# Layer 2 of a four-layer graph kernel: rel times (x Wvᵀ), with transposes by VectorE and DMA

## The chip, the cores and the metric

The kernel runs on one core of a Trainium2 chip. The metric is the device time in microseconds (us); each quoted time of the kernel is the median of several runs. All data and all matrix products are fp32.

## The reference, cut to what matters

There are 128 graphs of 128 nodes with 512 features. Four layers follow one another, each closed by a layer norm. The change is in layer 2, and it also touches how layer 3 moves its attention matrix.

```python
# layer 0: x = layernorm(x + norm_adj (x W0) + bias)
# layer 1: W1 = W2 = adj, so its term is constant over a row of x; the layer norm
# takes it out, and all that is left is a factor on the variance (the 1 + EPS of step vaw)
# layer 2
q = x @ Wq.T;  k = x @ Wk.T;  v = x @ Wv.T
rel = adj.T[None] * (q @ k.transpose(0, 2, 1))
rel = rel / norm(rel, axis=2, keepdims=True)
x = layernorm(x + rel @ v)
# layer 3
h = x @ W;  s1 = h @ a[:512];  s2 = h @ a[512:]
e = leaky_relu(s1[:, :, None] + s2[:, None, :], 0.2) * adj
att = softmax(e, axis=2)
x = layernorm(x + elu(att @ h + beta * h))
```

## The kernel before, in words

The 128 graphs go through in 32 groups of four (`GB = 4`). A group's `x` is one tile of 128 partitions (nodes) by 4 graphs by 512 features and stays in SBUF from its load to its store.

**The big products.** Each layer has products of a group's 512 rows with a 512x512 weight: `w` (layer 0), `z` (layer 2, x times gq = Wq^T Wk, giving the left factor of rel), `v` (layer 2, with Wv^T) and `k` (layer 3). Class `Product` (the matmul is line 525) does each in seven half-size products of 2x2 blocks instead of eight. They are numbered 1, 2, 5, 7, 6, 3, 4 in order of execution, need sums of blocks of the left operand (tile `S`, four sums) and of the weight (made once), and are combined afterwards by adds: `d` steps on VectorE (line 417), `t` and `c` copies out of PSUM on ScalarE (line 414), `u` steps on GpSimd (line 420). One product is 28 matmuls of 256 columns; in fp32 each shows as two records, so 56 passes.

**The left operands.** The product contracts over features, so x must stand with features on the partitions. Class `Left` gets that free of charge: `y` is x^T nadj^T, `u` is x^T rel^T and `v` (of steps `h`) is x^T att^T, each in 16 matmuls of 128 columns (line 581; 32 passes), with x as the stationary operand. Class `Squares` gives x^T itself for `z`: VectorE transposes 32x32 blocks (`xt`, line 480), then `xd` issues 16 DMAs of 64 KB that put the blocks in place (line 491). The sums of `y` and `x` are made by GpSimd (`sy`, `sx`), those of `u` and `v` by VectorE straight from PSUM (`su`, `sh`).

**Layer 2 before.** `r` makes rel from z and x^T (line 669, 16 matmuls); `rm` multiplies by adj^T; `sq` and `rp` give the row norms; `rs` scales rel by them on ScalarE; `rt` transposes rel on TensorE through PSUM (line 699) and `crt` copies it out; `u` is x^T rel^T; then the product `v` with Wv^T is added onto x.

**Layer 3 before.** `sc` makes the scores s1 and s2 on VectorE; `pe` spreads s2 over the partitions by four TensorE transposes (line 725); `pl`, `ej`, `ei`, `ex`, `rd`, `so` make the softmax; `at` transposes it on TensorE (line 764); `cat` (on VectorE) copies it out and adds beta times the identity; `h` and product `k` follow, and the elu steps `ee`, `em`, `ea`.

**The order.** It is written out as three strings: `HEAD` for the first groups, `TURN` repeated once for each group, and `TAIL` for the last. `5.w1` is step `w1` of group 5, counted from a base that grows by one at each turn. Each engine, and SyncE's DMA queue (SP) with them, executes its own share of the list strictly in that order; a step that waits holds all later ones of its engine. TensorE's order in a turn of before is `z w rt r pe u v at y h k`, for groups one to four apart. PSUM gives six rotating banks to these products; in SBUF the transposed left operands (tag `aT`) rotate over three buffers.

Of the kernel before, what the change touches and what calls it, by code (L numbers as in the profile page):

```python
# [48 lines left out]
FIRST = 5  # L50
LAST = -4
# [4 lines left out]
0.dw7 0.bi00 0.w3 0.tw 0.bi11 1.ld 0.w4 0.bi01 0.uw10 0.dw3 s.g0 0.uw01 0.dw4 0.uw11 0.stw0  # L56
0.stw1 s.g1 s.cg0 0.stw2 0.stw3 s.s30 0.vaw s.q00 0.pow s.g2 s.cg1 s.q01 0.nbw s.q02 0.apw0
s.q03 0.apw1 2.ld 3.ld 0.xt0 4.ld 0.apw2 s.q10 s.g3 0.apw3 0.xt1 s.cg2 0.xt2 0.xt3 s.q11 0.xd
s.q12 1.y10 s.cg3 s.q13 1.y00 1.cy10 s.sg0 1.y11 1.cy00 s.sg2 s.sg1 1.y01 1.cy11 s.sg3 1.w1
1.cy01 s.bi 1.sy0 1.w2 s.s32 1.dw1 1.sy1 1.w5 1.dw2 1.sy2 s.s31 1.w7 1.dw5 1.sy3 1.w6 s.s33  # L60
1.dw7 1.bi10 1.w3 1.tw 0.sx0 0.sx1 1.w4 1.dw3 0.sx2 0.z1 1.dw4 1.bi00 0.z2 0.cz1 0.sx3 1.bi11
0.z5 0.dz2 1.bi01 0.z7 0.cz5 1.uw10 0.z6 1.uw01 0.dz7 1.uw11 1.stw0 0.z3 0.tz 1.stw1 0.uz11
1.stw2 0.z4 1.stw3 0.dz3 2.y10 1.vaw 0.dz4 1.pow 2.y00 2.cy10 2.bi10 1.nbw 2.y11 2.cy00 1.apw0
2.y01 2.sy1 1.apw1 1.xt0 0.r0 1.apw2 1.xt1 2.bi00 0.r1 1.apw3 1.xt2 0.r2 2.bi11 2.cy01 1.xt3
2.cy11 0.r3 2.bi01 2.w1 1.xd 0.rm 2.sy0 0.sq0 0.sq1 2.w2 2.dw1 0.sq2 2.sy2 0.sq3 0.rp 2.w5 2.dw2
2.sy3 0.rs0 0.rs1 2.w7 2.dw5 0.rs2 0.rs3 2.w6 2.dw7 2.w3 2.tw 2.uw01 2.w4 2.uw10 2.dw3 2.stw0
2.uw11 0.rt 2.dw4 1.z1 0.crt 2.stw1 1.sx0 2.stw2 1.z2 1.cz1 1.sx1 2.stw3 2.vaw 1.sx2 1.z5 1.dz2
2.pow 1.z7 1.cz5 1.sx3 2.nbw 2.apw0 2.apw1 2.xt0 1.z6 1.dz7 2.apw2 2.xt1 2.apw3 1.z3 2.xt2 1.tz
2.xt3 1.uz11 2.xd 1.z4 1.dz3 0.u10 1.dz4 0.u00 0.cu10 0.u11 0.cu00 0.su1 0.u01 0.cu11 0.su0 1.r0
0.cu01 0.su2 1.r1 0.su3 1.r2 1.r3 s.t0 1.rm s.t1 s.ct0 s.t2 s.ct1 s.t3 s.ct2 s.wa s.ct3 1.sq0  # L70
s.sv0 1.sq1 0.v1 s.sv2 1.sq2 1.sq3 s.sv1 1.rp s.sv3 0.v2 0.dv1 2.sx0 1.rs0 1.rs1 1.rs2 0.v5
0.dv2 1.rs3 2.sx1 2.sx2 0.v7 0.dv5 2.sx3 0.v6 0.dv7 0.v3 0.tv 0.uv01 0.v4 0.uv10 0.dv3 0.stv0
0.uv11 1.rt 0.dv4 1.crt 0.stv1 1.u10 0.stv2 1.u00 1.cu10 0.stv3 1.u11 1.cu00 0.vav 1.su1 0.pov
1.u01 1.cu11 1.su0 2.z1 1.cu01 0.nbv 1.su2 0.apv0 1.su3 0.apv1 2.z2 0.sc00 2.cz1 0.sc01 0.apv2
2.z5 0.sc10 0.apv3 0.sc11 2.z7 0.sc20 2.cz5 0.sc21 0.sc30 2.z6 2.dz7 0.sc31 2.z3 2.tz 2.dz2
2.uz11 2.z4 2.dz3 0.pe 2.dz4 2.r0 0.pl0 0.pl1 2.r1 0.pl2 0.pl3 2.r2 0.ej 0.ei 2.r3 0.ex0 1.v1
2.rm 0.ex1 2.sq0 2.sq1 1.v2 1.dv1 2.sq2 2.sq3 0.ex2 2.rp 1.v5 0.ex3 1.dv2 2.rs0 0.rd 0.so 2.rs1
2.rs2 1.v7 1.dv5 2.rs3 1.v6 1.dv7 1.v3 1.tv 1.uv01 1.v4 1.uv10 1.dv3 1.stv0 1.uv11 0.at 1.dv4
2.rt 3.y10 0.cat 2.crt 1.stv1 3.y00 3.cy10 3.bi10 1.stv2 3.y11 3.cy00 3.bi00 1.stv3 3.y01 3.cy11
1.vav 3.sy0 0.h10 3.cy01 0.h00 0.ch10 3.sy1 0.h11 0.ch00 3.sy2 0.sh1 0.h01 0.ch11 0.sh0 2.u10  # L80
0.ch01 3.bi11 0.sh2 2.u00 2.cu10 0.sh3 3.sy3 2.u11 2.cu00 2.su1 2.u01 3.bi01 2.cu11 2.su0 3.w1
2.cu01 1.pov 2.su2 2.su3 3.w2 3.dw1 1.nbv 1.apv0 3.w5 3.dw2 1.apv1 1.sc00 1.apv2 1.sc01 3.w7
1.apv3 3.dw5 1.sc10 3.w6 3.dw7 1.sc11 3.w3 1.sc20 3.tw 3.uw01 1.sc21 1.sc30 3.w4 3.uw10 3.dw3
1.sc31 3.uw11 4.y10 3.dw4 4.y00 4.cy10 3.stw0 4.bi10 4.y11 3.stw1 4.cy00 4.bi00 4.y01 3.stw2
4.cy11 0.k1 3.stw3 4.sy0 4.cy01 3.vaw 3.pow 0.k2 0.ck1 4.sy1 3.nbw 3.apw0 0.k5 3.apw1 0.dk2
4.sy2 3.xt0 3.apw2 0.em00 3.apw3 0.k7 3.xt1 4.sy3 0.ck5 3.xt2 0.ee00 4.bi11 3.xt3 0.k6 0.dk7
4.bi01 0.k3 0.tk 0.ea00 0.uk11 0.k4 0.dk3 0.ee01 0.em01 0.ee11 0.em11 1.pe 3.xd 4.w1 1.pl0 0.dk4
1.pl1 0.ea01 1.pl2 1.pl3 0.ea11 4.w2 0.ee10 4.dw1 1.ej 4.w5 0.em10 1.ei 0.ea10 1.ex0 4.w7 1.ex1
4.dw5 1.ex2 0.stk0 1.ex3 4.w6 4.dw7 1.rd 0.stk1 4.w3 4.tw 1.so 0.stk2 4.uw01 4.w4 0.stk3 4.uw10
4.dw2 0.vak 3.z1 3.sx0 4.dw3 4.dw4 3.sx1 4.stw0 3.z2 3.cz1 4.stw1 3.sx2 3.z5 3.dz2 0.pok 3.sx3  # L90
0.nbk 3.z7 3.cz5 0.apk0 4.uw11 0.apk1 0.fin0 3.z6 3.dz7 0.apk2 0.fin1 4.stw2 0.apk3 0.fin2
4.stw3 3.z3 3.tz 0.fin3 4.vaw 3.uz11 3.z4 3.dz3 4.pow 4.nbw 2.v1 5.ld 3.dz4 4.apw0 4.apw1 4.xt0
2.v2 4.apw2 2.dv1 4.xt1 4.apw3 4.xt2 2.v5 4.xt3 2.dv2 2.v7 2.dv5 2.v6 2.dv7 2.v3 2.tv 2.uv01
2.v4 2.uv10 2.dv3 2.stv0 2.uv11 3.r0 4.xd 2.dv4 3.r1 2.stv1 3.r2 2.stv2 3.r3 2.stv3 1.at 2.vav
3.rm 2.pov 5.y10 1.cat 3.sq0 5.y00 5.bi10 5.cy10 2.nbv 3.sq1 5.y11 5.cy00 5.bi00 5.y01 3.sq2
5.cy11 5.sy1 1.h10 5.cy01 3.sq3 1.h00 5.sy0 1.ch10 1.h11 1.ch00 3.rp 2.apv0 1.sh1 1.h01 1.ch11
2.sc00 5.sy2 1.k1 1.ch01 1.sh0 3.rs0 5.bi11 1.sh2 3.rs1 3.rs2 1.k2 2.sc01 1.ck1 4.sx0 3.rs3
1.sh3 2.apv1 1.k5 1.dk2 4.sx1 2.apv2 2.sc10 2.apv3 2.sc11 4.sx2 1.k7 1.ck5 2.sc20 1.ee00 5.sy3
2.sc21 1.k6 1.dk7 4.sx3 2.sc30 1.k3 1.tk 2.sc31 5.bi01 1.em00 1.k4 1.dk3 1.uk11 1.ee01 1.ea00
4.z1 1.dk4 1.ee11 1.em01 4.z2 4.cz1 1.em11 1.ea01 1.em10 4.z5 1.ee10 4.dz2 1.ea11 4.z7 4.cz5  # L100
1.ea10 1.stk0 4.z6 4.dz7 1.stk1 1.stk2 4.z3 4.tz 4.uz11 1.stk3 1.vak 4.z4 4.dz3 1.pok 1.nbk
1.apk0 5.w1 4.dz4 1.apk1 1.fin0 1.apk2 1.fin1 5.w2 5.dw1 1.apk3 1.fin2 1.fin3 5.w5 5.dw2 5.w7
5.dw5 6.ld 5.w6 5.dw7 5.w3 5.tw 5.uw01 5.w4 5.uw10 5.dw3 5.stw0 5.uw11 3.rt 5.dw4 4.r0 3.crt
5.stw1 4.r1 5.stw2 4.r2 5.stw3 4.r3 5.vaw 5.pow 2.pe 4.rm 3.u10 2.pl0 5.nbw 4.sq0 3.u00 3.cu10
2.pl1 3.u11 3.cu00 2.pl2 3.u01 3.su1 3.cu11 3.v1 2.pl3 3.su0 3.cu01 3.su2 5.apw0 2.ej 3.v2
5.apw1 3.dv1 5.apw2 3.su3 5.apw3 3.v5 2.ei 4.sq1 5.xt0 2.ex0 3.dv2 3.v7 2.ex1 3.dv5 2.ex2 5.xt1
2.ex3 3.v6 5.xt2 4.sq2 4.sq3 3.dv7 4.rp 2.rd 5.xt3 3.v3 3.tv 2.so 5.xd 4.rs0 4.rs1 3.uv01 4.rs2
3.v4 4.rs3 3.uv10 3.dv3 3.stv0 2.at 3.uv11 6.y10 2.cat 6.y00 3.dv4 6.cy10 6.bi10 3.stv1 6.y11
6.cy00 6.bi00 3.stv2 6.y01 6.cy11 3.stv3 2.h10 6.cy01 6.sy0 3.vav 2.h00 2.ch10 6.sy1 2.h11
2.ch00 2.sh1 6.sy2 2.h01 2.ch11 2.sh0 2.k1 2.ch01 3.pov 2.sh2 2.sh3 6.sy3 2.k2 2.ck1 3.nbv  # L110
3.apv0 5.sx0 3.apv1 3.sc00 2.k5 5.sx1 3.apv2 3.sc01 3.apv3 3.sc10 5.sx2 2.k7 2.ck5 3.sc11 3.sc20
6.bi11 2.k6 2.dk7 5.sx3 3.sc21 3.sc30 2.k3 2.tk 6.bi01 3.sc31 2.dk2 2.uk11 2.k4 2.dk3 2.ee00
2.em00 2.ee11
"""
TURN = """
4.z1 1.dk4 1.em11 1.em01 4.z2 4.cz1 1.ea00 1.ea11 1.ee01 4.z5 4.dz2 1.ee10 1.em10 1.ea01 4.z7
4.cz5 1.ea10 1.stk0 4.z6 4.dz7 1.stk1 4.z3 1.stk2 4.tz 4.uz11 1.stk3 4.z4 4.dz3 1.vak 1.pok 5.w1
4.dz4 1.nbk 1.apk0 5.w2 5.dw1 1.apk1 1.fin0 1.apk2 1.fin1 1.apk3 5.w5 1.fin2 5.dw2 1.fin3 5.w7
5.dw5 5.w6 5.dw7 6.ld 5.w3 5.tw 5.uw01 5.w4 5.uw10 5.dw3 5.stw0 5.uw11 3.rt 5.dw4 4.r0 3.crt
5.stw1 4.r1 5.stw2 4.r2 5.stw3 4.r3 5.vaw 5.pow 2.pe 4.rm 3.u10 2.pl0 5.nbw 4.sq0 3.u00 3.cu10  # L120
2.pl1 3.u11 3.cu00 2.pl2 3.u01 3.su1 3.cu11 3.v1 2.pl3 3.su0 3.cu01 3.su2 5.apw0 2.ej 3.v2
5.apw1 3.dv1 5.apw2 3.su3 5.apw3 3.v5 2.ei 4.sq1 5.xt0 2.ex0 3.dv2 3.v7 2.ex1 3.dv5 2.ex2 5.xt1
2.ex3 3.v6 5.xt2 4.sq2 4.sq3 3.dv7 4.rp 2.rd 5.xt3 3.v3 3.tv 2.so 5.xd 4.rs0 4.rs1 3.uv01 4.rs2
3.v4 4.rs3 3.uv10 3.dv3 3.stv0 2.at 3.uv11 6.y10 2.cat 6.y00 3.dv4 6.cy10 6.bi10 3.stv1 6.y11
6.cy00 6.bi00 3.stv2 6.y01 6.cy11 3.stv3 2.h10 6.cy01 6.sy0 3.vav 2.h00 2.ch10 6.sy1 2.h11
2.ch00 2.sh1 6.sy2 2.h01 2.ch11 2.sh0 2.k1 2.ch01 3.pov 2.sh2 2.sh3 6.sy3 2.k2 2.ck1 3.nbv
3.apv0 5.sx0 3.apv1 3.sc00 2.k5 5.sx1 3.apv2 3.sc01 3.apv3 3.sc10 5.sx2 2.k7 2.ck5 3.sc11 3.sc20
6.bi11 2.k6 2.dk7 5.sx3 3.sc21 3.sc30 2.k3 2.tk 6.bi01 3.sc31 2.dk2 2.uk11 2.k4 2.dk3 2.ee00
2.em00 2.ee11
"""  # L130
TAIL = """
# [59 lines left out]
6.stk3 7.uk11 7.dk2 7.k4 6.vak 7.ee00 7.dk3 6.pok 7.ee11 7.em11 6.nbk 7.dk4 6.apk0 7.em00 6.apk1  # L191
6.fin0 7.em01 6.apk2 6.fin1 7.ea00 6.apk3 6.fin2 7.ea11 7.ee01 6.fin3 7.em10 7.ee10 7.ea01
7.ea10 7.stk0 7.stk1 7.stk2 7.stk3 7.vak 7.pok 7.nbk 7.apk0 7.apk1 7.fin0 7.apk2 7.fin1 7.apk3
7.fin2 7.fin3
"""


@with_exitstack
def kernel(
# [213 lines left out]
    def copy(o, i):  # L413
        nc.scalar.copy(o, i)  # L414
# [465 lines left out]
```

## Time and profile before

| What | us |
|---|---|
| median of 3 runs (2092.33 to 2092.88) | 2092.64 |
| the profiled execution | 2092.67 |
| its span, first to last instruction | 2090.8 |
| TensorE busy | 2067.4 |
| VectorE busy | 1474.3 |
| GpSimd busy | 928.3 |
| ScalarE busy | 917.9 |
| DMA queue of SP, share of 16 engines | 17.9% |
| mean granted TensorE clock | 0.997 |

1.87 us of the profiled execution lie outside the span. The profile page has the busy time of each engine, the chain of work that ended last (followed back from the last instruction; each step is either what released the next or the instruction before it on its engine), groups of equal instructions with their busy and idle time, and DMA issues with the time from issue to landing. The timeline lists runs of equal instructions in order. A group's "mean ns of one" is the latency of one instruction; where instructions overlap, as matmuls do, the time that one adds is the length of a run divided by its count.

### The profile page before, as it was taken

The page shows a single profiled execution, that of the slowest core. Times are in us where ns is not written, and L with a number is a line of the kernel's source. Part 1 is how long each engine was busy: PE and PEld are TensorE (multiplying, and loading weights), DVE is VectorE, ACT ScalarE, POOL GpSimd, SP SyncE. Part 2 cuts the span into 40 slices and gives each one's busy share as a digit, 9 for nine tenths or more (in the row PEclk, how much of TensorE's full clock was granted, in tenths as well). Part 3 has the DMA queues.
Part 4 walks back from the last instruction along what each step waited for, and adds up shares of the span by engine and source line. Part 5 has one row for each costly group of instructions (what it writes and reads, how often), then busy time and mean ns, then how long its engine had stood idle before and what let it go on. Part 6 is the DMA issues. An engine that isn't in the chain of part 4 may idle for free.

```text
span 2090.8 us, 32011 instructions
## 1 busy us (share of the span) xinstructions
PE 2067.4 (99%) x11706; PEld 1871.8 (90%) x11706; DVE 1474.3 (71%) x2984; ACT 917.9 (44%) x1961; POOL 928.3 (44%) x776
## 2 busy tenths in 40 slices
PE   9999999999999999999999999999999999999996
PEld 6989999999998989999999989899999999899886
DVE  5568766777766677666777666776767766678777
ACT  2344444435444444444354444444443444444455
POOL 5636553354543445533545434455335454346311
PEclk9999999999999999999999999999999999999998
DMA  7101221121121111211212212112112122121102
GB/s 238 35 7 21 61 61 57 45 62 28 54 61 46 56 42 41 61 55 47 62 24 58 61 45 57 42 40 61 54 48 61 21 61 61 44 59 21 26 16 81
DMA packets 112445, 108.85 MB, mean 52 GB/s; under 512 B 11040, under 2 KB 76704, under 8 KB 112288
## 3 DMA queue, kind: packets, MB, share of 16 engines
q1 hardware_dynamic: 112288, 106.80, 17.9%
q8 instruction: 93, 1.52, 0.3%
q14 instruction: 64, 0.52, 0.1%
HBM read 39.65 MB, written 33.55 MB: 35 GB/s over the span
## 4 chain that ended last, share of the span: by engine, by line
PE 98%; DVE 1%; issue 0%; ACT 0%; POOL 0%; DMA 0%; POOLq 0%; ACTq 0%; DVEq 0%
PE p_v L525 19%; PE p_z L525 19%; PE p_w L525 18%; PE p_k L525 18%; PE pu L581 6%; PE pr L669 5%; PE py L581 5%; PE pv L581 5%; PE pg L355 1%; PE prt L699 1%; PE pe L725 1%; PE pat L764 1%; ACT x L629 0%; DVE st_v L607 0%; DMA adj_sb<-in_adj_dram 0%
## 5 line engine op out<-in xcount | busy, mean ns | idle before, releaser
L417 DVE TENSOR_TENSOR x<-p_w,x 128x512 f32<-128x512 f32 x192 | 132.0, 688 | 204.7 <-PE p_w L525 124.0
L420 POOL TENSOR_TENSOR x<-x,t_w 128x512 f32<-128x512 f32 x96 | 119.3, 1270 | 257.7 <-ACT t_w L414 256.9
L417 DVE TENSOR_TENSOR x<-p_v,x 128x512 f32<-128x512 f32 x192 | 130.1, 678 | 84.5 <-POOL x L420 59.6
L710 DVE SCALAR_TENSOR_TENSOR prod<-x,wa_bc 128x512 f32<-128x512 f32 x256 | 161.0, 681 | 21.5 <-ACT x L629 21.5
L420 POOL TENSOR_TENSOR zT<-zT,t_z 128x512 f32<-128x512 f32 x32 | 40.6, 1268 | 293.8 <-ACT t_z L414 288.3
L525 PE MATMUL p_w<-w_t,S_y 128*128 128x256 f32 x768 | 171.0, 379 | 0.0
L525 PE MATMUL p_v<-wvT_t,S_u 128*128 128x256 f32 x768 | 171.0, 379 | 0.0
L525 PE MATMUL p_k<-w_t,S_v 128*128 128x256 f32 x768 | 171.0, 379 | 0.0
L525 PE MATMUL p_z<-S_x,gq_t 128*128 128x256 f32 x768 | 171.0, 379 | 0.0
L420 POOL TENSOR_TENSOR x<-x,t_v 128x512 f32<-128x512 f32 x96 | 119.2, 1269 | 112.4 <-ACT t_v L414 112.4
L420 POOL TENSOR_TENSOR x<-x,bias_bc 128x512 f32<-128x512 f32 x128 | 162.5, 1281 | 13.2 <-PE py L581 12.3
L525 PEld LDWEIGHTS p_v<-wvT_t,S_u 128*128 128x128 f32 x768 | 146.2, 190 | 19.6
L525 PEld LDWEIGHTS p_w<-w_t,S_y 128*128 128x128 f32 x768 | 146.2, 190 | 19.6
L525 PEld LDWEIGHTS p_k<-w_t,S_v 128*128 128x128 f32 x768 | 146.2, 190 | 19.6
L525 PEld LDWEIGHTS p_z<-S_x,gq_t 128*128 128x128 f32 x768 | 146.2, 190 | 19.6
L424 POOL TENSOR_TENSOR r_n<-n,minus_half 128x4 f32<-128x4 f32 x32 | 32.3, 1009 | 281.7 <-ACT sq L685 281.7
L629 ACT ACTIVATE x<-x,nb,r_k 128x512 f32<-128x512 f32 x128 | 94.4, 803 | 101.8 <-DVE nb L623 101.8
L581 PE MATMUL py<-nadjT,x 128*128 128x128 f32 x1024 | 121.9, 279 | 0.4 <-DVE nadjT L348 0.4
L581 PE MATMUL pu<-relT,x 128*128 128x128 f32 x1024 | 119.9, 276 | 2.4 <-ACT relT L414 2.4
L581 PEld LDWEIGHTS py<-nadjT,x 128*128 128x128 f32 x1024 | 119.3, 195 | 1.4 <-DVE nadjT L348 0.8
L581 PE MATMUL pv<-attT,x 128*128 128x128 f32 x1024 | 119.6, 275 | 0.4 <-DVE attT L417 0.4
L581 PEld LDWEIGHTS pu<-relT,x 128*128 128x128 f32 x1024 | 116.9, 192 | 3.2 <-ACT relT L414 3.1
(1028 smaller groups left out, 4729.0 us busy)
## 6 DMA issues: line engine op xcount, KB each, us to landing
out_dram<-x SPq DMA_DIRECT2D x128, 256.0 KB, 2.1
x<-in_x_dram SPq DMA_DIRECT2D x31, 1024.0 KB, 5.2
x<-in_x_dram SPq DMA_DIRECT2D x2, 512.0 KB, 4.6
w<-in_L_gnn_weight_dram SPq DMA_DIRECT2D x1, 1024.0 KB, 7.1
wq_sb<-in_L_gnn_Wq_dram SPq DMA_DIRECT2D x1, 1024.0 KB, 10.4
wk_sb<-in_L_gnn_Wk_dram SPq DMA_DIRECT2D x1, 1024.0 KB, 12.4
wv_sb<-in_L_gnn_Wv_dram SPq DMA_DIRECT2D x1, 1024.0 KB, 15.4
w<-in_L_gnn_W_dram SPq DMA_DIRECT2D x1, 1024.0 KB, 16.9
```

The lines of the kernel that those rows point to most:

```text
L355: nc.tensor.matmul(wide(pg), lhsT=wq_sb[:, ec, bass.ts(gc, P)], rhs=wk_sb[:, ec, :], start=(ec == 0), stop=(ec == KC - 1),)
L417: nc.vector.tensor_tensor(o, a, b, f)
L420: nc.gpsimd.tensor_tensor(o, a, b, f)
L424: nc.gpsimd.tensor_tensor(r, v, minus_half, ALU.pow)
L525: nc.tensor.matmul(ps[:, j, :], lhsT=lhsT, rhs=rhs, start=(i not in ONTO and j == 0 and kc == 0), stop=(j == 1 and kc == 1), skip_group_ch ...
L581: nc.tensor.matmul(o, lhsT=self.x_chunk(b, kc), rhs=rhs, start=True, stop=True)
L629: nc.scalar.activation(xt, xt, AF.Identity, bias=self.nb[k][:, b : b + 1], scale=self.rstd[k][:, b : b + 1],)
L669: nc.tensor.matmul(self.pr[:, b, :], lhsT=self.zT[:, fc, b, :], rhs=self.xT.chunk(b, fc), start=(fc == 0), stop=(fc == KC - 1),)
L699: nc.tensor.transpose(self.prt[:, b, :], self.rel[:, b, :], ident)
L710: nc.vector.scalar_tensor_tensor(prod, self.x[:, b, :], 1.0, wide(wa_bc[k]), ALU.mult, ALU.mult, accum_out=self.s[:, k, b : b + 1],)
L725: nc.tensor.transpose(self.pse[:, b, :], s2, ident)
L764: nc.tensor.transpose(self.pat[:, b, :], self.e[:, b, :], ident)
```

## The change

Layer 2 is computed as rel (x Wv^T) in place of (rel x) Wv^T. The product `v` now takes x^T as its left operand, the same tile and the same four sums `S` as `z`, and its result goes to a tile of its own (`whole["v"]`, tag `vC`). Then four matmuls `f`, one per graph, with rel^T as stationary operand and 512 columns of that tile moving, give the layer's output, and `fa` on VectorE scales it by the row norm and adds it onto x in one instruction. Steps `u`, `cu`, `su`, `rs`, `uv10` and `uv01` are gone.

rel and att are transposed without TensorE: VectorE transposes 32x32 blocks (`rt`, `at`), one DMA writes the result to DRAM (`wr`, `aw`), and four DMAs of 32 partitions read it back in place (`cr`, `cat`). s2 is written to DRAM (`pw`) and read back spread over all partitions (`pe`). beta times the identity is now added in `so`, four instructions. x^T is laid out so that two feature chunks alternate element by element: the sums read contiguous blocks, and a matmul that takes one chunk reads every second element. The DMAs of `xd` move runs of 64 elements where they moved runs of 128. Tiles of pool `mid` have one buffer where they had two. The three order strings are new; 21 turns lie between a head of four groups and a tail of seven, where 23 lay between five and four.

```diff
 TURN = """
+4.z1 5.cy01 2.em01 2.em10 4.z2 4.cz1 3.pe 2.ea11 5.sy0 2.ee01 4.z5 4.dz2 5.sy1 4.z7 4.cz5 2.ea01
+3.pl0 5.sy2 2.stk0 2.ee10 2.stk1 4.z6 3.pl1 5.bi10 3.pl2 4.dz7 3.pl3 3.ej 4.z3 4.tz 2.ea10 3.ei
+4.uz11 4.z4 4.dz3 3.ex0 5.sy3 3.ex1 2.stk2 3.ex2 4.r0 2.stk3 3.ex3 5.bi00 4.dz4 4.r1 3.rd 5.bi11
+2.vak 4.r2 4.r3 3.so0 2.pok 3.so1 5.w1 3.so2 3.so3 4.rm 5.bi01 3.at 4.sq0 5.w2 4.sq1 5.dw1 3.aw
+4.sq2 2.nbk 4.sq3 2.apk0 5.w5 4.rp 5.dw2 2.apk1 2.fin0 2.apk2 2.fin1 4.rt 5.w7 2.apk3 3.cat
+5.dw5 5.w6 5.dw7 4.wr 5.w3 5.tw 2.fin2 5.uw01 2.fin3 5.w4 5.uw10 5.dw3 4.cr 5.stw0 5.uw11 3.h10
+5.dw4 3.h00 5.stw1 3.ch10 3.h11 5.stw2 3.ch00 7.ld 3.h01 5.stw3 3.ch11 3.sh0 4.v1 3.ch01 5.vaw
+3.sh1 5.pow 3.sh2 4.v2 4.cv1 5.nbw 3.sh3 5.apw0 5.apw1 5.xt0 4.v5 4.dv2 5.apw2 5.xt1 5.apw3 4.v7
+5.xt2 4.cv5 5.xt3 4.v6 4.dv7 4.v3 4.tv 4.uv11 4.v4 4.dv3 4.f0 5.xd 4.dv4 4.f1 4.fa0 4.stv0 4.f2
+4.fa1 4.f3 4.fa2 3.k1 4.fa3 4.stv1 3.k2 3.ck1 4.stv2 4.stv3 3.k5 3.dk2 4.vav 3.ee00 3.em00 4.pov
+3.k7 3.ck5 3.ea00 4.nbv 4.apv0 3.k6 3.dk7 4.apv1 4.sc00 4.apv2 4.sc01 3.k3 4.apv3 4.sc10 5.sx0
+3.tk 4.sc11 3.k4 5.sx1 4.sc20 4.sc21 5.sx2 6.y10 4.sc30 6.y00 6.cy10 4.sc31 3.uk11 3.dk3 6.y11
+4.pw 6.cy00 5.sx3 3.dk4 3.ee11 6.y01 6.cy11 3.em11
 """
...
-    mid = ctx.enter_context(tc.tile_pool(name="mid", bufs=2))
+    mid = ctx.enter_context(tc.tile_pool(name="mid", bufs=1))
+    dram = ctx.enter_context(tc.tile_pool(name="dram", bufs=2, space=bass.MemoryType.DRAM))
...
         def square(self, b, x):
             nc.vector.transpose(
-                self.u[:, b].rearrange("p q k r -> p k q r"),
-                x.rearrange("p (k q a) -> p k q a", k=KC, q=4),
+                self.u[:, :, b].rearrange("p h t r e -> p h e t r"),
+                x.rearrange("p (h e t a) -> p h e t a", h=2, e=2, t=4),
             )
         def move(self):
-            self.aT = big.tile([P, GB, 4, KC, 32], F32, tag="aT", name=f"{self.name}T")
+            self.aT = big.tile([P, 2, GB, P, 2], F32, tag="aT", name=f"{self.name}T")
             for q in range(4):
                 for to in range(4):
-                    nc.sync.dma_start(out=self.aT[rows(to), :, q], in_=self.u[rows(q), :, to])
+                    nc.sync.dma_start(
+                        out=self.aT[rows(to), :, :, rows(q), :], in_=self.u[rows(q), :, :, to]
+                    )
...
+    def across(o, u, name):
+        d = dram.tile([P, 4, P], F32, tag="sq", name=f"d_{name}")
+        nc.sync.dma_start(out=d, in_=u)
+        yield
+        by_t = d.rearrange("(q i) t x -> t i q x", q=4)
+        for t in range(4):
+            nc.sync.dma_start(out=o[rows(t)], in_=by_t[t])
+        yield
...
-                "v": Product(f"v_{g}", self.u, "v"),
+                "v": Product(f"v_{g}", self.xT, "v"),
...
-        def rs(self, b):
-            r = self.rel[:, b, :]
-            nc.scalar.activation(r, r, AF.Copy, scale=self.rnorm[:, b : b + 1])
-
         def rt(self):
-            self.prt = bank(f"prt_{self.g}")
-            for b in range(GB):
-                nc.tensor.transpose(self.prt[:, b, :], self.rel[:, b, :], ident)
-
-        def crt(self):
-            self.relT = mid.tile([P, GB, P], F32, tag="relT", name=f"relT_{self.g}", bufs=1)
-            copy(self.relT, self.prt)
+            self.ru = mid.tile([P, 4, 32, GB], F32, tag="ru", name=f"ru_{self.g}")
+            nc.vector.transpose(
+                self.ru.rearrange("p t r b -> p b t r"),
+                self.rel.rearrange("p b (t a) -> p b t a", t=4),
+            )
+        def wr(self):
+            self.relT = mid.tile([P, 4, 32, GB], F32, tag="relT", name=f"relT_{self.g}")
+            flat = lambda t: t.rearrange("p t r b -> p t (r b)")
+            self.way = across(flat(self.relT), flat(self.ru), f"r_{self.g}")
+            next(self.way)
+        def cr(self):
+            next(self.way)
+        def f(self, b):
+            nc.tensor.matmul(
+                self.pf[b],
+                lhsT=self.relT.rearrange("p q r b -> p b (q r)")[:, b],
+                rhs=self.whole["v"][:, b, :],
+                start=True,
+                stop=True,
+            )
+        def fa(self, b):
+            xt = self.x[:, b, :]
+            nc.vector.scalar_tensor_tensor(
+                xt, self.pf[b], self.rnorm[:, b : b + 1], xt, ALU.mult, ALU.add
+            )
...
+        def pw(self):
+            self.d = dram.tile([P, GB], F32, tag="s2", name=f"d_s_{self.g}")
+            nc.sync.dma_start(out=self.d, in_=self.s[:, 1, :])
         def pe(self):
-            self.pse = bank(f"pe_{self.g}")
-            for b in range(GB):
-                s2 = self.s[:, 1, b : b + 1].to_broadcast([P, P])
-                nc.tensor.transpose(self.pse[:, b, :], s2, ident)
+            self.s2 = mid.tile([P, P, GB], F32, tag="ru", name=f"s2_{self.g}")
+            flat = self.d.rearrange("j b -> (j b)").partition_broadcast(P)
+            nc.sync.dma_start(out=self.s2.rearrange("p j b -> p (j b)"), in_=flat)
...
-        def so(self):
-            tt(self.e, self.e, self.rden.unsqueeze(2).to_broadcast([P, GB, P]), ALU.mult)
+        def so(self, b):
+            nc.vector.scalar_tensor_tensor(
+                self.e[:, b, :], self.e[:, b, :], self.rden[:, b : b + 1], beta_i, ALU.mult, ALU.add
+            )
         def at(self):
-            self.pat = bank(f"pat_{self.g}")
-            for b in range(GB):
-                nc.tensor.transpose(self.pat[:, b, :], self.e[:, b, :], ident)
+            self.au = mid.tile([P, 4, GB, 32], F32, tag="ru", name=f"au_{self.g}")
+            nc.vector.transpose(
+                self.au.rearrange("p t b r -> p b t r"),
+                self.e.rearrange("p b (t a) -> p b t a", t=4),
+            )
         def cat(self):
-            self.attT = mid.tile([P, GB, P], F32, tag="attT", name=f"attT_{self.g}", bufs=1)
-            tt(self.attT, self.pat, beta_i.unsqueeze(1).to_broadcast([P, GB, P]))
+            next(self.way)
```

## The prediction

> **What bounds the kernel now.** I read the page's busy times first, then the chain of work that ended last, then the stages of one turn.
>
> ```profile
> PE 2067.4 (99%) x11706; PEld 1871.8 (90%) x11706; DVE 1474.3 (71%) x2984; ACT 917.9 (44%) x1961; POOL 928.3 (44%) x776
> ...
> PE 98%; DVE 1%; issue 0%; ACT 0%; POOL 0%; DMA 0%; POOLq 0%; ACTq 0%; DVEq 0%
> ```
>
> TensorE is in the chain for 98% of the span, and no other engine comes near it. A busy TensorE alone proves little, as matmuls are pipelined; so I look for gaps. All waits of TensorE's matmuls that the list of waits shows come to under 9 us, most of it before the first product. Then I take the pieces of the chain in order of time, one turn:
>
> ```profile
> 1043.33 3.57 PE pr L669 x32
> ...
> 1050.91 12.09 PE p_v L525 x56
> 1063.44 3.57 PE py L581 x32
> 1067.01 3.57 PE pv L581 x32
> 1070.58 12.09 PE p_k L525 x56
> 1082.67 12.09 PE p_z L525 x56
> 1094.76 12.09 PE p_w L525 x56
> ```
>
> The p_v of the next turn starts at 1114.87, so a turn lasts 63.96 us. It is full: four products of 12.09 are 48.36, four stages of 3.57 (r, u, y, h) are 14.28, three sets of transposes at 0.434 are 1.30: 63.94. So a microsecond less of TensorE work is a microsecond less of time, as long as nothing else becomes late. The price of a pass is the run divided by its count: 12.09/56 = 216 ns at 256 columns, 3.57/32 = 112 ns at 128. At 512 columns the setup's product gives it:
>
> ```profile
> 23.68 13.73 PE pg L355 x32
> ```
>
> 13.73/32 = 429 ns.
>
> [...] 2.0 to 2.1 us from issue to landing for the stores of 256 KB and the moves of 64 KB. [...] loads of 190 ns lie inside passes that follow each other at 216 ns.
>
> **The change part by part, for one group.** TensorE, on the path:
>
> - removed: u, 32 passes, 3.57 us; the transposes rt, pe and at, 3 x 0.434 = 1.30 us. Sum 4.87.
> - added: f, four matmuls of 512 columns, 8 passes x 0.429 = 3.43 us. The same columns stream as in u; what is saved there is the fixed part of 24 passes, 0.14 us.
> - kept: w, z, v, k, y, h, r at their lengths. z and r now read x^T at every second element, and v loads its weights so. Unknown cost; from below nothing, since the same number of columns streams. From above, half rate: 12.09 + 3.57 = 15.7 us. I take zero [...]. The weight loads for v could last 216 ns before they show, and f's, at every fourth element, 429 ns.
>
> Net -1.44 us, so a turn of 62.5. For 32 groups: 32 x 1.44 = 46.1 us.
>
> VectorE, beside TensorE: removed are four sums su (0.61 us each as one follows another, from the timeline), two of six adds dv, so and cat: 8 x 0.61 = 4.9. Added are four fa and two transposes at 0.61 (3.7) and four so of 128 columns. No such row exists: at least 0.15 us each, as for the smallest operations, at most the 0.61 of four times the size; 0.6 to 2.4, I take 1.1. Net -0.1: it stays near 45 us of a turn of 62.5, against 45.16 of 63.95. The transposes write with gaps of 8 or 16 bytes; at double time they add 6 x 0.61 = 3.7 us, still below 50. ScalarE loses four cu and crt (0.49 each) and four rs (0.32), gains two cv: -2.8. GpSimd loses two uv: -2.5. Neither bounds anything, so these are worth nothing.
>
> SP's queue gains 12 DMAs a group (wr, aw, pw, pe one each, cr and cat four each) beside the 16 of xd, four stores and one load:
>
> ```profile
> 995.80 11.06 SPq L491 DMA_DIRECT2D x_16T<-sq_x  x16
> ...
> 1032.47 2.45 SPq L638 DMA_DIRECT2D out_dram<-x  x4
> ```
>
> An issue takes about 0.7 us, so 33 take 23 us of 62.5. What matters is when they land. I set t = 0 at z1 of a turn; TensorE then runs z to 12.1, r to 15.7, w to 27.8, h to 31.3, v to 43.4, f to 46.9, k to 59.0, y to 62.5.
>
> - rel: r ends at 15.7, rm and rt by about 20.5 (rt waits for the DMA aw to let go of tag ru), wr lands at 23, cr, behind two stores, by 26 to 28. f starts at 43.4: 15 us to spare. f0 also needs dv3 and f2 dv4; each has one product step (1.73) or two f (1.7) of cover.
> - att: f ends at 46.9, so fa, the statistics, apv and sc on VectorE end at about 59.5 (dk7 waits until k7 at 53.8). pw and pe, one issue and 2.0 us each, land at about 64.5, which is 2.0 of the next turn. pl stands behind cz5 (5.3) on ScalarE anyway, so this round trip is hidden with 3 us. ej, ei, ex, rd, so end at 14.6; at waits behind rm (r ends at 15.7) and ends at 17.0; aw lands at 19.1; cat issues behind stores fin0 and fin1, held by apk0 and apk1, and lands at 24.4. h starts at 27.8: 3.4 us to spare. This is the tightest chain. A late cat delays h and everything behind it on TensorE.
> - x^T: xd now waits for v4, because x^T of the group before is in use until then (three buffers aT, three tiles in a turn). So 43.5 to 54.5 for 16 issues, landed at 56.5; sx at 1.25 us each. z1 starts at 62.5: 6 us to spare, and z5 needs the first sum only at 66.
>
> The single buffers of pool mid cost nothing as I see it: t is used once a product, 12 us apart; prod and sq by one engine in order; only ex makes each ee wait for the ea before it, 0.6 us on ScalarE, which is more than half idle. Of the new waits, rt behind aw holds VectorE's dw5, dw7 and dw3; xd behind v4 holds only pw on SP, which is not ready before 59.5.
>
> Head and tail do the same steps in other orders. Before, TensorE starts at 5.57, and after its last product 20.8 us of elu, norm and stores follow; both stay. In the tail the last group has, between f and h, 47.0 us of TensorE steps (h and k of three groups) as cover, where a turn has 43.4, but 43 us of VectorE steps where a turn has 30. I allow 1.5 us for gaps, with 0 and 10 as ends.
>
> **Sum.** 2092.67 (profiled execution; 2090.8 span and 1.87 around it; the median, 2092.64, is the same) - 46.1 + 1.5 = **2048 us**.
>
> **The rivals.**
>
> *The DMA round trip through DRAM is late.* If att lands d us after 27.8, or the last groups wait, TensorE stands still by d each turn. For: 3.4 us is little, and the write and the reads are new forms; reads of 512-byte runs could take longer than 2.0. Against: xd moves runs of 512 bytes with 2.0 us. With each of aw and cat at 4.5 us, 0.9 of aw's delay is hidden behind fin1, and cat lands at 24.4 + 1.6 + 2.5 = 28.5: 0.7 late, 31 x 0.7 = 22 us, 2070. It decides from 3.4 us on.
>
> *x^T arrives late; this one ends slower.* Runs of 64 elements double the pieces of each xd DMA. If its issues double too, to a period of 1.4 us, 15 x 1.4 + 2.5 = 23.5 us after 43.4 is 66.9, and z1 is 4.4 us late in each turn: 31 x 4.4 = 136, 2184 us. It costs nothing up to a period of (19.0 - 2.5)/15 = 1.1 us and eats the whole gain from (20.4 - 2.5)/15 = 1.2. Against: the number of pieces does not set the issue time here; a store of 128 pieces takes 0.33 us, a load of 512 pieces 0.39, an xd of 128 pieces 0.6. DMA engines are busy 43% in that stretch, so twice the packets would just fit.
>
> *The strided reads cost.* z and r at half rate: 32 x 15.7 = 502 us, about 2550. The gain is gone at 1.44/15.7, a 9% slowdown. [...]
>
> *The work was not on the path.* If TensorE's passes waited for weight loads, fewer of them would not help: 2092. Against: the turn adds up from passes to 0.02 us.
>
> **How the numbers follow.** Forecast 0.72, with its own range 2043 (1.5 us of allowance and some of the old gaps gone, 0.14 us more from f) to 2060; late round trip 0.15 (2060 to 2085); x^T late 0.06; strided reads 0.05; not on the path 0.02. About 0.2%, 4 us, is what a measurement tells from no change. Faster: 0.72 + 0.15 = 0.87, less 0.01 for a round trip worse than 2088, 0.86; same 0.02 + 0.01 = 0.03; slower 0.06 + 0.05 = 0.11. For 8 in 10 the range takes in the forecast and the better half of the late round trip: 2043 to 2073.
>
> **What would show it.** Right: a turn of 62.5 us, z and r at 216 and 112 ns a pass, runs of f at 3.43, no transposes of rel, e and s on TensorE, VectorE at 45 us a turn. Wrong: TensorE waiting on attT before h (round trip), on x^T or S_x before z (xd's issue above 1.1 us), longer passes in p_z and pr alone (strides), or gaps in the tail above 10 us.

## The result and the profile after

| What | before | after |
|---|---|---|
| median, us | 2092.64 | 2068.68 (2068.12 to 2069.11) |
| ratio to before, 95% interval | | 0.9885 (0.9868 to 0.9903) |
| profiled execution, us | 2092.67 | 2068.12 |
| its span, us | 2090.8 | 2066.2 |
| one turn, us | 63.96 | 63.18 |

The change gains 24 us. The forecast was 2048 with a range of 2043 to 2073, a gain of 44.6. So the sign and the range held, and close to half of the gain is missing. The first two lines to read on the page after are again the busy times and the shares of the chain of work that ended last.

```profile
PE 2041.6 (99%) x10554; PEld 1800.8 (87%) x10554; DVE 1610.6 (78%) x3048; ACT 844.1 (41%) x1737; POOL 915.1 (44%) x712
...
PE 95%; DVE 2%; issue 1%; ACT 1%; DMA 0%; SPq 0%; POOL 0%; POOLq 0%; ACTq 0%; DVEq 0%
```

TensorE is still busy for 99% of the span, with a tenth fewer instructions; VectorE rose by 136 us. The missing gain is therefore not idle time of TensorE. The list of waits confirms it: TensorE's matmuls wait 7.7 us in all, none of it for attT or relT. So the time must lie in the length of TensorE's pieces. The chain of the kernel after, in order of time, has for one turn (start, length, engine, what it writes, line, count of passes):

```profile
1004.17 3.57 PE pv L617 x32
1007.74 12.10 PE p_v L564 x56
1023.28 12.09 PE p_k L564 x56
1035.37 3.57 PE py L617 x32
1038.94 12.69 PE p_z L564 x56
1051.63 3.63 PE pr L703 x32
1055.26 12.09 PE p_w L564 x56
1067.35 3.57 PE pv L617 x32
```

The stretch without a line, 1019.84 to 1023.28, is f with 3.44 us. Two pieces are longer than before: p_z has 12.69 instead of 12.09 us, and pr has 3.63 instead of 3.57. These are the two that now read x^T at every second element. The product p_v, which takes every second element as weights, kept its length within 0.01 us. The groups of equal instructions say the same of single instructions (busy us, then the mean ns of one):

```profile
L564 PE MATMUL p_z<-S_x,gq_t 128*128 128x256 f32 x768 | 179.2, 387 | 0.0
...
L564 PE MATMUL p_v<-wvT_t,S_x 128*128 128x256 f32 x768 | 171.0, 379 | 0.0
```

Both are 768 matmul records of 256 columns with the same S_x; only the role of S_x differs. As the moving operand it costs 179.2 us, as weights 171.0, which is also what p_z cost before.

The account closes: 12.69 - 12.09 = 0.60 and 3.63 - 3.57 = 0.06 make 0.66 us a turn, and 32 x 0.66 = 21.1 us. The profiled execution of before less the 46.1 us of the forecast plus these 21.1 is 2092.67 - 46.1 + 21.1 = 2067.7; measured is 2068.12.

### The profile page after: what moved, and what is told of

Same layout as the page of the kernel before. It is cut to its first block, busy times and chain, and to the rows that moved or that the text cites. A ratio compares the mean times of both kernels' runs of the same rounds, so it can differ in the third digit from the quotient of the medians.

```text
span 2066.2 us, 29797 instructions
## 1 busy us (share of the span) xinstructions
PE 2041.6 (99%) x10554; PEld 1800.8 (87%) x10554; DVE 1610.6 (78%) x3048; ACT 844.1 (41%) x1737; POOL 915.1 (44%) x712
## 4 chain that ended last, share of the span: by engine, by line
PE 95%; DVE 2%; issue 1%; ACT 1%; DMA 0%; SPq 0%; POOL 0%; POOLq 0%; ACTq 0%; DVEq 0%
PE p_z L564 19%; PE p_v L564 19%; PE p_w L564 18%; PE p_k L564 17%; PE pr L703 6%; PE py L617 5%; PE pv L617 5%; PE pf L746 5%; PE pg L379 1%; DVE x L852 0%; DMA x<-in_x_dram 0%; SPq L518 0%; ACT x L665 0%; DVE prod L765 0%; DVE st_k L643 0%
## 5 line engine op out<-in xcount | busy, mean ns | idle before, releaser
L564 PE MATMUL p_z<-S_x,gq_t 128*128 128x256 f32 x768 | 179.2, 387 | 0.0
L564 PE MATMUL p_w<-w_t,S_y 128*128 128x256 f32 x768 | 171.0, 379 | 0.0
L564 PE MATMUL p_v<-wvT_t,S_x 128*128 128x256 f32 x768 | 171.0, 379 | 0.0
L448 POOL TENSOR_TENSOR r_v<-v,minus_half 128x4 f32<-128x4 f32 x32 | 43.7, 1366 | 287.0 <-DVE v L652 286.8
L564 PEld LDWEIGHTS p_z<-S_x,gq_t 128*128 128x128 f32 x768 | 144.1, 188 | 29.9
L564 PEld LDWEIGHTS p_v<-wvT_t,S_x 128*128 128x128 f32 x768 | 150.8, 196 | 14.9
L844 ACT ACTIVATE ex<-C_k 128x512 f32<-128x512 f32 x128 | 80.8, 631 | 146.3 <-DVE x L852 85.1
L848 DVE SCALAR_TENSOR_TENSOR x<-C_k,x 128x512 f32<-128x512 f32 x128 | 136.0, 1096 | 0.0
L441 DVE TENSOR_TENSOR C_v<-p_v,t_v 128x512 f32<-128x512 f32 x64 | 44.3, 692 | 113.9 <-PE p_v L564 113.9
L852 DVE SCALAR_TENSOR_TENSOR x<-ex,x 128x512 f32<-128x512 f32 x128 | 124.9, 976 | 10.2 <-ACT ex L844 5.2
L444 POOL TENSOR_TENSOR C_v<-C_v,t_v 128x512 f32<-128x512 f32 x32 | 40.5, 1266 | 201.1 <-ACT t_v L438 196.1
L665 ACT ACTIVATE x<-x,nb,r_v 128x512 f32<-128x512 f32 x128 | 94.4, 804 | 69.2 <-DVE nb L659 69.2
L617 PEld LDWEIGHTS pv<-attT,x 128*128 128x128 f32 x1024 | 119.4, 192 | 2.3 <-issue 0.5
```

The costliest lines, as they stand in the source:

```text
L441: nc.vector.tensor_tensor(o, a, b, f)
L444: nc.gpsimd.tensor_tensor(o, a, b, f)
L448: nc.gpsimd.tensor_tensor(r, v, minus_half, ALU.pow)
L564: nc.tensor.matmul(ps[:, j, :], lhsT=lhsT, rhs=rhs, start=(i not in ONTO and j == 0 and kc == 0), stop=(j == 1 and kc == 1), skip_group_ch ...
L617: nc.tensor.matmul(o, lhsT=self.x_chunk(b, kc), rhs=rhs, start=True, stop=True)
L665: nc.scalar.activation(xt, xt, AF.Identity, bias=self.nb[k][:, b : b + 1], scale=self.rstd[k][:, b : b + 1],)
```

## The experiments

My theory after these readings: the change gains its 1.44 us a turn as forecast, and reading x^T with a step of two elements as the moving operand takes 0.66 of them back. Rivals: the longer passes come from something else in the new schedule (the DMA traffic, VectorE), and the step is innocent; or the price of a step is a fixed one per pass, or one that grows evenly with the stretch of memory that a pass reads.

### e1_plain: the change without the steps

```diff
-            self.aT = big.tile([P, 2, GB, P, 2], F32, tag="aT", name=f"{self.name}T")
-            self.s = big.tile([P, 4, 2, P, 2], F32, tag="S", name=f"S_{self.name}")
+            self.aT = big.tile([P, GB, KC, P], F32, tag="aT", name=f"{self.name}T")
+            self.s = big.tile([P, 4, 2, 2, P], F32, tag="S", name=f"S_{self.name}")
...
         def chunk(self, b, kc):
-            return self.aT[:, kc // 2, b, :, kc % 2]
+            return self.aT[:, b, kc]
```

The transposes and the DMAs of xd follow this layout (runs of 32 elements).

> The kernel after, with x^T laid out so that a chunk's 128 columns are contiguous (its DMAs then move runs of 32 elements instead of 64). Theory (strided reads): every pass of p_z is back at 216 ns and of pr at 112, the turn goes from 63.18 to 62.5 us, and the time from 2068.7 to 2068.7 - 32 x 0.66 = 2047.5. Rival (the longer passes of p_z and pr come from the traffic beside them: DMA, GpSimd's sums): passes stay at 227 ns, 2068.7 or, with more DMA pieces, above. Rival (x^T late): with runs of 128 bytes xd's issue grows above 1.1 us and TensorE waits for x^T before z.

Measured: 2079.29 us (2078.71 to 2079.39), ratio to before 0.9935 (0.992 to 0.995): slower than after by 10.6 us. Every pass is short again, but the list of waits of this kernel has a new first line (total us, times, longest):

```profile
PE pr L701 <- DVE C_z L441: 17.9, 46, 0.6
PE pt_nadj L368 <- DVE nadj L364: 4.5, 1, 4.5
```

r waits, in its middle, for the last two adds of z (dz3 and dz4, which write C_z). From the start of r at 1059.13 to the start of w at 1064.00 are 4.87 us instead of 3.57: 1.30 are lost, of which only 0.76 are marked as waits. The reason is on VectorE. Its timeline in this kernel, ahead of dz3:

```profile
1056.32 0.68 DVE L441 TENSOR_TENSOR e<-e,adj_sb 128x512 f32<-128x512 f32 x1
1056.92 1.76 DVE L850 SCALAR_TENSOR_TENSOR x<-ex,x 128x512 f32<-128x512 f32 x1
1058.60 0.67 DVE L800 TENSOR_REDUCE nmax<-e 128x4 f32<-128x512 f32 x1
1059.20 0.68 DVE L441 TENSOR_TENSOR C_z<-p_z,t_z 128x512 f32<-128x512 f32 x1
```

The elu step ea10 takes 1.76 us. In the kernel after, the same step takes 0.69:

```profile
1048.70 0.69 DVE L852 SCALAR_TENSOR_TENSOR x<-ex,x 128x512 f32<-128x512 f32 x1
```

What differs is GpSimd's add uz11 (a step of z) beside it. First the timeline of GpSimd in e1_plain, then in the kernel after:

```profile
1056.55 1.58 POOL L444 TENSOR_TENSOR C_z<-C_z,t_z 128x512 f32<-128x512 f32 x1 [3.03 <-ACT t_z L438]
```

```profile
1048.70 1.83 POOL L444 TENSOR_TENSOR C_z<-C_z,t_z 128x512 f32<-128x512 f32 x1 [3.39 <-ACT t_z L438]
```

In e1_plain uz11 starts 0.37 us ahead of ea10, and ea10 is the one that is stretched. In the kernel after both start at 1048.70, ea10 keeps its 0.69, and uz11 takes 1.83 where an undisturbed add of this size takes 1.27. So in each of the two traces one of the two instructions is stretched: ea10 where uz11 began first, uz11 where both began together. In e1_plain ea10 ends 0.55 us behind the end of uz11, and 1.07 of its 1.76 us are more than the 0.69 of the kernel after. uz11, which with 1.58 us is 0.31 longer than 1.27, began while the VectorE step ahead of ea10 (first line above, both inputs in SBUF) was running, from 1056.32 to 1057.00. A shorter z makes ScalarE's tz and so uz11 earlier: uz11 starts 9.50 us after the first pass of z in e1_plain and 9.92 us after it in the kernel after, ea10 9.87 and 9.92 us. So in e1_plain uz11 comes first. The experiment thus changed two things in a turn: it removed 0.66 us of passes and added 1.3 us of waiting. It doesn't yet show what the step alone costs. The rival of a late x^T showed nothing: in a full turn no pass of z waits for it.

### e2_before_stride: the steps without the change

The kernel before, with only its x^T laid out in alternating chunks.

```diff
-                self.aT = big.tile([P, GB, 4, KC, 32], F32, tag="aT", name=f"{self.name}T")
+                self.aT = big.tile([P, 2, GB, P, 2], F32, tag="aT", name=f"{self.name}T")
...
         def chunk(self, b, kc):
-            return self.aT[:, b, :, kc]
+            return self.aT[:, kc // 2, b, :, kc % 2]
```

> The kernel before with only the layout of x^T taken from the kernel after (z and r read every second element, xd moves runs of 64). Theory (strided reads): p_z passes at 227 ns and pr at 113.5 there too, a turn of 63.95 + 0.66, 2092.6 + 21 = 2113.8. Rival (traffic of the new kernel): passes stay at 216, 2092.6.

Measured: 2114.61 us (2113.3 to 2114.72), ratio 1.0102 (1.0085 to 1.0119), 21.9 us slower than before. The schedule, the products and the DMA count are those of before; z and r alone are longer. Its chain has them with the lengths of the kernel after:

```profile
1030.14 12.69 PE p_z L530 x56
...
1055.36 3.63 PE pr L674 x32
```

That rules out the new schedule and its traffic as the cause of the longer passes: the step costs 21.9 / 32 = 0.68 us a group by itself. Nor do the shorter runs that xd moves in this layout make the passes longer: in e1_plain they are shorter still, and the passes take 216 ns.

### e3_stride4: all four chunks alternate

One chunk of x^T is now every fourth element. That holds for r and for the 24 of z's 56 passes that read x^T itself; the sums keep a step of two.

```diff
-            self.aT = big.tile([P, 2, GB, P, 2], F32, tag="aT", name=f"{self.name}T")
+            self.aT = big.tile([P, GB, P, KC], F32, tag="aT", name=f"{self.name}T")
...
         def chunk(self, b, kc):
-            return self.aT[:, kc // 2, b, :, kc % 2]
+            return self.aT[:, b, :, kc]
```

> The kernel after with all four chunks alternating: 24 of the 56 passes of p_z and all of pr read every fourth element (one per 16 bytes), the other 32 passes of p_z, on the sums, every second; xd moves runs of 128 elements again. [...] 248 ns a pass at every fourth, 0.77 + 0.34 + about 0.2 us a turn instead of 0.66, near 2089. [...] up to twice the pass, 2300. If it is a fixed price for any gapped operand: all at 227, 2068.7.

Measured: 2371.71 us (2371.04 to 2372.1), ratio 1.1332 (1.1316 to 1.1349). The chain of this kernel, one turn:

```profile
1014.42 12.61 PE p_v L562 x56
...
1046.14 18.08 PE p_z L562 x56
1064.22 7.25 PE pr L701 x32
```

p_z grew by 18.08 - 12.69 = 5.39 us, pr by 3.62, p_v by 0.51: 9.52 a turn and 305 in 32, of 303.0 measured (2371.71 - 2068.68). By TensorE's timeline the 16 passes of z on x^T take 7.20 us, 450 ns each, where a step of two takes 227 and contiguous elements 216; r's pass takes 7.25/32 = 227 ns, where it took 113 and 112. So a fixed price per pass (227 for all) is out, and so is a price that grows evenly with the stretch of memory read, which is the 248 ns of the expectation: 10.7 ns for the second KB, 32 for three more. A step of two costs 5%, one of four the double, 450 ns against 216 and 227 against 112. As weights, a step of four costs too: 16 passes of p_v take 3.84 us, 240 ns each instead of 216; their loads last 326 ns where a step of two has 196.

### e4_scores_by_pe: one set of transposes put back

s2 is spread by TensorE as before, and the two DMAs pw and pe are gone.

```diff
         def pw(self):
-            self.d = dram.tile([P, GB], F32, tag="s2", name=f"d_s_{self.g}")
-            nc.sync.dma_start(out=self.d, in_=self.s[:, 1, :])
+            pass
         def pe(self):
-            self.s2 = mid.tile([P, P, GB], F32, tag="ru", name=f"s2_{self.g}")
-            flat = self.d.rearrange("j b -> (j b)").partition_broadcast(P)
-            nc.sync.dma_start(out=self.s2.rearrange("p j b -> p (j b)"), in_=flat)
+            self.pse = bank(f"pe_{self.g}")
+            for b in range(GB):
+                s2 = self.s[:, 1, b : b + 1].to_broadcast([P, P])
+                nc.tensor.transpose(self.pse[:, b, :], s2, ident)
```

> The kernel after with one part undone: the scores s2 are spread by four TensorE transposes again, without the two DMAs. Theory (TensorE has no gaps in the kernel after either): 32 x 0.434 = 13.9 us more, 2082.6. Rival (the round trip through DRAM costs something elsewhere, or the 0.434 us had been hidden): less, down to 2068.7 or below.

Measured: 2081.47 us (2080.72 to 2082.63), ratio 0.9946 (0.9932 to 0.9961): 12.8 us slower than after, 0.40 a group. The transposes stand in the turn between z2 and z5 with 0.43 us, and no wait of a full turn went away with the DMAs. So the removed transposes were worth what they took on TensorE, and the DMA that replaced this one was free.

### e5_plain_order and e6_after_order: the order of VectorE

e5 is e1_plain with ea10 moved behind dz3, and two statistics steps behind dz4, in the 21 turns and the two like them that open the tail (the 46 waits of e1_plain are two in each of these 23). e6 is the same move in the kernel after.

```diff
-3.pl0 5.sy2 2.stk0 2.ee10 2.stk1 4.z6 3.pl1 5.bi10 3.pl2 4.dz7 3.pl3 3.ej 4.z3 4.tz 2.ea10 3.ei
-4.uz11 4.z4 4.dz3 3.ex0 5.sy3 3.ex1 2.stk2 3.ex2 4.r0 2.stk3 3.ex3 5.bi00 4.dz4 4.r1 3.rd 5.bi11
+3.pl0 5.sy2 2.stk0 2.ee10 2.stk1 4.z6 3.pl1 5.bi10 3.pl2 4.dz7 3.pl3 3.ej 4.z3 4.tz 3.ei 4.uz11
+4.z4 4.dz3 2.ea10 3.ex0 5.sy3 3.ex1 3.ex2 4.r0 4.dz4 2.stk2 2.stk3 3.ex3 5.bi00 4.r1 3.rd 5.bi11
```

> e1_plain with one VectorE step of each turn moved: ea10, which in e1 takes 1.76 us because GpSimd's uz began 0.4 us before it, now stands behind dz3, and the statistics stk2 and stk3 behind dz4. Theory (r waited for dz3 and dz4 only because that one step collides with GpSimd): the gaps of 1.3 us before r go, a turn of 62.5 us, about 2050. Rival (VectorE's steps between k and r are too many in any order once z is short): the gap moves or stays, near 2079.

> The kernel after, strided reads kept, with the same step moved. Theory (its turns have no gap at all, so VectorE's order is not on the path): 2068.7, no change. Rival (the move itself is worth time): faster, up to the 29 us that e5 should gain on e1.

e5 took 2049.0 us (2047.36 to 2049.49), ratio 0.9792 (0.9778 to 0.9807). VectorE's timeline shows that ea10 is still long, 1.63 us, now beside the next add of GpSimd (sy3, 1041.90 to 1043.16), but it stands behind dz3:

```profile
1041.48 0.69 DVE L441 TENSOR_TENSOR C_z<-p_z,t_z 128x512 f32<-128x512 f32 x1
1042.09 1.63 DVE L850 SCALAR_TENSOR_TENSOR x<-ex,x 128x512 f32<-128x512 f32 x1
1043.64 0.68 DVE L441 TENSOR_TENSOR C_z<-p_z,t_z 128x512 f32<-128x512 f32 x1
```

And the chain of the same kernel, whose pieces follow one another without a gap, has for a turn:

```profile
996.25 3.57 PE pv L615 x32
...
1031.01 12.09 PE p_z L562 x56
1043.10 3.57 PE pr L701 x32
...
1058.76 3.57 PE pv L615 x32
```

From pv to pv it is 62.51 us, the forecast's 62.5, with p_z and pr at their old lengths. e6 took 2068.22 us (2067.89 to 2068.31), ratio 0.9885 (0.9871 to 0.99): with the steps left in, the order gains nothing. So the gain of e5 over e6, 19.2 us on the same chip, is that of the layout without steps. Over 32 groups 21 were due; e5 has a wait of 1.9 us before its first z, which e6 has at 0.6. e5 is the fastest version of this study.

### e7_att_hops: a longer round trip for att

Two copies from DRAM to DRAM are put between the write of att and its reads.

```diff
+        for hop in range(2 if name[0] == "a" else 0):
+            d2 = dram.tile([P, 4, P], F32, tag=f"hop{hop}", name=f"d{hop}_{name}")
+            nc.sync.dma_start(out=d2, in_=d)
+            d = d2
         by_t = d.rearrange("(q i) t x -> t i q x", q=4)
```

> The kernel after with att's round trip through DRAM made longer by two copies from DRAM to DRAM, each waiting for the one before, about 2.5 us each. The trace of the kernel after has att landed 3.4 us ahead of h. Theory (this slack is real and the round trip is hidden): 5.0 - 3.4 = 1.6 us late in each turn, 28 x 1.6 = 45 us, 2114. Rival (att's landing already sets something else): the whole 5 us a turn, 2210. If the slack is larger than read: 2068.7.

Measured: 2142.01 us (2139.22 to 2144.24), ratio 1.0239 (1.0222 to 1.0256), 73.3 us slower than after, which is between the two values expected. In its DMA queue (start, length of the run of issues) the hops and the reads of one turn are:

```profile
1029.87 3.51 SPq L541 DMA_DIRECT2D d_a<-d_a  x2
1035.79 1.76 SPq L545 DMA_DIRECT2D attT<-d_a  x4
```

In TensorE's timelines w starts at 1025.10 here, so the reads are issued 10.69 us behind it; in the kernel after it is 5.09 us (1055.10 and 1060.19). So they are late by 5.60 us, not by the 5 that I had estimated. The last 8 passes of w start at 1035.46 in that turn, so at 0.216 us each h was due at 1037.19. The timeline has:

```profile
1039.30 5.44 PE L621 MATMUL pv<-attT,x 128*128 128x128 f32 x32 [1.95 <-DMA attT<-d_a]
1044.57 3.62 PE L568 MATMUL p_v<-wvT,x_15T 128*128 128x256 f32 x16
```

h starts 2.11 us late: of 5.60 us the schedule swallowed 3.5, near the 3.4 that the forecast had. But h itself then takes 5.27 us up to the start of v instead of 3.57. The windows of this kernel show why (the last three columns are the granted clock as a share of the full one, DMA share and GB/s):

```profile
1034.00:1037.20 3.20, 3.20 (x16) 2.61 (x14) 1.21 (x2) 0.52 (x1) 2.54 (x3) 1.00 0.33 101
1039.30:1040.20 0.90, 0.90 (x8) 0.90 (x9) 0.86 (x3) 0.00 (x0) 0.00 (x0) 1.00 1.00 378
1040.30:1043.60 3.30, 3.30 (x18) 3.30 (x17) 0.26 (x2) 1.17 (x2) 0.00 (x0) 0.50 0.52 131
1043.80:1048.00 4.20, 4.20 (x25) 3.91 (x24) 2.97 (x7) 2.66 (x5) 1.02 (x1) 1.00 0.63 239
```

The granted clock is 1.00 ahead of the pause and for the first 1.0 us behind it, then 0.50 for 3.41 us (windows of 0.05 us put this stretch at 1040.27 to 1043.68), and then 1.00 again. Half the clock for 3.41 us loses 1.7 us, and that is what h is longer. In the chain's pieces h is 5.1 or 5.4 us long behind 9 of the 24 waits and 3.81 behind the other 15. The mean clock agrees with a stretch behind each of the 9 and one in the tail: it is 0.989 instead of 0.997, about 17 us of 2139, which is ten times 1.7. The 0.24 us by which the other 15 are longer than 3.57 stay open.

The length of a pause alone does not tell which kind follows: by the chain, one of 1.88 us (up to 578.04) has an h of 5.44 us behind it, one of 2.26 us (up to 1372.55) an h of 3.81. What decides is not shown here.

The sum: 47.4 us of waits plus 20.1 us of longer h (15 x 0.24 + 1.57 + 8 x 1.87) are 67.5. In the tail a wait of k grew by 2.4 us, and 16 passes of k behind it last 5.41 us in the chain instead of about 3.5; I count this as one more stretch, 1.7 us. That makes 71.6 of the 72.7 us between the profiled executions.

## Why the prediction was right, and what it got wrong

**What bounds the kernel: right.** TensorE filled the turn before and fills it after. The gain came out of its pieces alone, and e5's turn of 62.51 us meets the forecast's 62.5 without any term fitted.

**The removed work: right.** u and the transposes are gone from the turn. e4 put 0.43 us of transposes back and lost 0.40 a group. So the rival "not on the path" falls.

**f: right.** 3.44 us against 3.43. Its weights, every fourth element, showed no cost in passes of 429 ns (3.44/8 = 430), as forecast. In passes of 216 ns they do: e3's p_v, with 240.

**z and r at every second element: the step that failed.** The forecast took zero, the lower of its two bounds. In the trace of before no pass of z or r reads every second element, so zero was an assumption of mine that nothing had shown. Measured: 227 instead of 216 ns at 256 columns, 113.5 instead of 111.6 at 128; 0.66 us a turn, 21 us in all. The prediction had set the bounds zero and half rate, 0 and 15.7 us a turn; the true term lay at 4% of the way between them, and it was the largest error of the sum. The rival "the strided reads cost" had the cause and named its mark, "longer passes in p_z and pr alone", which is just what the trace showed, but with a size that ate half the gain, not all of it. The upper bound is reached only at a step of four: in e3 such passes take the double, 450 and 227 ns.

**Weights of v at every second element: right.** 12.10 against 12.09 us; the load takes 196 ns instead of 190 and hides in a pass of 216.

**VectorE: wrong, without effect on this kernel.** The forecast said that it "stays near 45 us of a turn"; the windows of one turn have 50.6. Two groups of the kernel after hold half of that:

```profile
L848 DVE SCALAR_TENSOR_TENSOR x<-C_k,x 128x512 f32<-128x512 f32 x128 | 136.0, 1096 | 0.0
...
L852 DVE SCALAR_TENSOR_TENSOR x<-ex,x 128x512 f32<-128x512 f32 x128 | 124.9, 976 | 10.2 <-ACT ex L844 5.2
```

These are the elu steps em and ea, which the change doesn't touch; before they took 707 and 700 ns. Four of each a turn make 4 x 0.39 + 4 x 0.28 = 2.7 us. They now run beside GpSimd's adds with both inputs in SBUF; that they are stretched by those is shown for ea10 by e1 and the kernel after, for the others only read from the timelines (ea at 1042.40 in the kernel after takes 1.77 us, beside an add from 1041.89 to 1043.62). The so of 128 columns took 0.56 us each, 2.24 for four, near my upper end of 2.4 where I took 1.1; in e1 and e5 the same four take 1.13. The transpose rt with gaps of 16 bytes took 1147 ns (1135 in e1), while the one of e, without gaps, took 701 and those of x with gaps of 8 bytes 693 (687 before). What I had missed is that VectorE's order matters before it is full: by the timelines of the kernel after, the adds dz3 and dz4 end 1.3 and 0.5 us ahead of the passes of r that e1 shows waiting for them. That cover was not in the prediction; in this order of VectorE it holds only because z is slow, and in e1 its loss cost 2079.29 - 2049.0 = 30 us (23 x 1.30 = 29.9).

**The DMA round trip of att: right, with its slack.** The queue of SP in the turn shown:

```profile
1014.02 10.39 SPq L518 DMA_DIRECT2D x_16T<-sq_x  x16
...
1056.63 0.32 SPq L537 DMA_DIRECT2D d_a<-au  x1
1058.73 1.04 SPq L674 DMA_DIRECT2D out_dram<-x  x2
1060.19 1.77 SPq L541 DMA_DIRECT2D attT<-d_a  x4
```

The last read is issued by 1061.96 and lands 2.0 us later, at 1064.0; h starts at 1067.35. That is the 3.4 us of the forecast. e7 shows that there is not much more, and that beyond it a pause can cost TensorE's clock as well (behind the pause shown, 0.50 for 3.41 us).

**x^T late: fell, for the reason given.** The 16 issues of xd take 10.39 us, 0.65 each, though each has twice the pieces; the sums begin in time. With four times the pieces (e1) they took 10.67.

**The tail: right.** Of the allowance of 1.5 us, 0.4 were needed (2068.12 - 2067.7).

So the prediction was right by its main account and lucky in its range: one term that it put at zero was 21 us, and the range reached there only for the sake of another rival. And had that term been zero, this order of the steps would not have given the forecast 2048 either: e1, which has short passes in the same order, took 2079.29 us, outside the range.

## What to carry to other kernels

A layout that serves two readers isn't free because each seems to lose little: multiply even 5%, as z lost here (227 against 216 ns), by every pass that reads it, and compare that with the gain before choosing the layout. Where one engine is full, look not only for its waits but for longer pieces of the same count. When a bound engine gets faster, the instructions of the others that were just in time no longer are; give the adds that feed it a place ahead of work that can wait. A mean of the clock over a long window can hide two states (in e7 it is 0.66 from 1039 to 1044 us, where shorter windows have 1.00 and 0.50), so make the windows shorter until the figure no longer changes.

## What the runs showed of the hardware

- fp32 passes with a step in the moving operand: 216, 227 and 450 ns at 256 columns for steps of one, two and four elements (e1, after, e3); 112, 113.5 and 227 ns at 128 columns. Why a step of two costs 10.7 ns at 256 columns and only 1.9 at 128 stays open.
- Weights at a step of four: passes of 256 columns at 240 ns instead of 216 (e3); at a step of two no cost in a product (12.10 against 12.09 us, after).
- A VectorE instruction with two SBUF inputs beside a GpSimd add of the same size: 1.76 us instead of 0.69 where GpSimd began first, ending 0.55 us behind the add (e1); the add took 1.83 instead of 1.27 where they began together (after).
- TensorE's clock (e7): behind a pause of 1.95 us it was granted 1.00 for 1.0 us, 0.50 for 3.41 us and then 1.00 again, a loss of 1.7 us. Of 24 pauses (2.0 us on average) 9 had an h of 5.1 or 5.4 us behind them, 15 one of 3.81.
- A 32x32 block transpose of 128x512 fp32 on VectorE: 0.69 to 0.70 us without gaps in what it writes (before, e1, after), 0.69 with gaps of 8 bytes (after), 1.13 to 1.15 with gaps of 16 bytes (e1, after).
- Twice and four times the pieces in a DMA of 64 KB left the time of 16 issues at 10.4 (after) and 10.7 us (e1), against 11.1 before.
